# Turning the rounded values by 32x32 blocks and plain DMAs, and reordering the writes of one DMA queue, in an attention and int8 layer on one core

## The chip, the core and the metric

The kernel runs on one core of a Trainium2 chip. The core has a matrix engine (PE; its weight loads are shown as a separate row, PEld), a vector engine (DVE), a scalar engine (ACT), a general engine (POOL) and a sync engine (SP), which here only issues DMAs. Each works through its own queue in order, and they meet by semaphores. The metric is device microseconds of one execution; the value that counts is the median of several runs.

## The reference

The input is 16 sequences of 256 tokens with 256 features. Everything is float32. Two layers follow each other, each on a layer-normalised input and added back to its residual:

```
x = x + attention(layernorm(x))     # 16 heads of 128, 4 key/value heads
x = x + int8_linear(layernorm(x))   # 256 -> 256, with a bias
```

In the attention a query sees the first 4 tokens (the sink) and the last 32 (the window). In the linear layer each token's 256 values are divided by their largest absolute value over 127 and rounded to whole numbers; the weight's rows likewise; the product of the whole numbers is scaled back, and the bias is added.

## The kernel before

**Units.** The attention of one sequence `n` is cut into 8 units `(n, g, t)`: 4 key/value heads `g` by two halves `t` of the tokens. There are 128 units, and the main loop goes through them one after the other. Below, "unit k" is unit k of a sequence, k = 0 to 7; "unit 125" and the like counts over all 128. Inside a unit PE does the scores (`pss`, `L560`), some of the output projection of earlier units (`py`, `L678`), weights times values of the unit two before (`po`, `L623`), and then queries for units to come (`pq`, `L527`). In every even unit a "chunk" of keys or values for coming units stands ahead of the queries: keys (`pk`, `L495`) in units 4 and 0, values (`pv`, `L507`) in units 6 and 2. All engines' instructions stay in the order in which the program writes them (`in_written_order`).

**Seven products.** Queries, keys, values and output projections are made by a Strassen scheme: seven 128x128 products where eight would be plain (on PE each float32 product is two instructions). Four products go into one PSUM bank and three into another (`REGION`). `LARGE_FIRST` writes the bank of four first, `SMALL_FIRST` the bank of three. For keys and values the bank of four comes from the pool `m`, which has two buffers, and the bank of three is one of two query banks `q0`, `q1`. A query uses both query banks; the combination of its products on DVE (`L306` to `L310`) frees its first bank after `L307`. For keys and values ACT copies the bank of three out first, then the bank of four (`both_banks`, `L323`), and POOL combines the copies.

**Softmax weights.** DVE scales, masks and normalises the scores, turns them in 32x32 blocks (`L582`), and SP writes them to DRAM (`zd`, `L584`). At the begin of the next unit SP reads them back in another order (`ad`, `L588`); PE takes them in `po` one unit later. The first units and the last six do this turning on PE instead (`ptd`, `L565`), and PE then takes the result one unit later and not two (`lag`).

**Values.** POOL's combined values are written to DRAM (`vd`, `L512`) in the unit of the chunk, and read back from there in the next unit by three reads (`vw`, `L448` to `L453`).

**Inputs.** The normalised input of a coming sequence is turned in two steps (`turned_by_blocks`, `L385`): DVE turns 32x32 blocks, four DMAs write them to DRAM (`L394`), and one unit later four DMAs read them back in an order that completes the turn (`L403`).

**The linear layer.** `ffn_steps` (`L695`) makes a list of steps. The table `slots` (`L880`) says how many units after the end of the sequence's attention each is written, and it has a row of its own for sequence 14; sequence 15 is treated apart (`last_steps`). The steps are statistics, normalisation, scale, `quantise` (DVE multiplies and adds a large constant, POOL clips in `L724` and subtracts the constant with a bf16 result in `L725`), `turn` (one transposing DMA from bf16 to bf16, `L728`) and `linear` (four bf16 products `pa` on PE, `L739`; two DVE instructions, `L744`; a POOL addition, `L745`; the write of the result, `L746`). In a steady sequence `turn` stands in unit 1 and `linear` in unit 2.

**Where a step lands.** A step under `small` is written at the end of its unit; under `begin`, at the start, directly behind the issue of `ad`; under `later`, behind the unit's softmax. From unit 125 on the `small` steps are written earlier: on DVE ahead of the unit's normalisation (`L605` and on), on PE ahead of `po`. `close` belongs to the last unit.

Of the kernel before, what the change touches and what calls it, by code (L numbers as in the profile page):

```python
# [9 lines left out]
FP = mybir.dt.float32  # L10
BF = mybir.dt.bfloat16
AF = mybir.ActivationFunctionType
ALU = mybir.AluOpType
# [21 lines left out]
def kernel(  # L35
# [12 lines left out]
    pe, dve, act, pool, sp = nc.tensor, nc.vector, nc.scalar, nc.gpsimd, nc.sync  # L48
    B, T, DM = x.shape
    P = 128  # L50
# [4 lines left out]
    NC = DM // P  # L55
    NT = T // P
# [4 lines left out]
    QB = 32  # L61
# [9 lines left out]
    SCALE = 1.0 / math.sqrt(D)  # L71

    const = ctx.enter_context(tc.tile_pool(name="const", bufs=1))
    xp = ctx.enter_context(tc.tile_pool(name="xp", bufs=5))
    p1 = ctx.enter_context(tc.tile_pool(name="p1", bufs=1))
    p2 = ctx.enter_context(tc.tile_pool(name="p2", bufs=2))
    p3 = ctx.enter_context(tc.tile_pool(name="p3", bufs=3))
# [192 lines left out]
    def products(p, factors, order=LARGE_FIRST):  # L270

        a, sa, b, sb = factors
        pairs = {
            1: (a[0][0], b[0][0]), 2: (a[0][1], b[1][0]), 6: (sa[1], sb[1]), 7: (sa[2], sb[2]),
            4: (a[1][1], sb[3]), 5: (sa[0], sb[0]), 3: (sa[3], b[1][1]),
        }
        for i in order:
            yield region(p, i), *pairs[i]

    SMALL_FIRST = (4, 5, 3, 1, 2, 6, 7)
    turn_of = [0]

# [62 lines left out]
    def factors(n, w, sums, pair):  # L348

        a = [[w[:, c, (2 * pair + e) * D : (2 * pair + e + 1) * D] for c in range(NC)] for e in range(2)]  # L350
        return (
            a, [sums[:, i, pair % 2] for i in range(4)],
            xn_blocks(n), [xn_sums[n][:, i] for i in range(4)],
        )
# [27 lines left out]
        dve.tensor_copy(xnT[n], pt)  # L382
        channels(n)

    def turned_by_blocks(n):  # L385


        z = p1.tile([P, NQ, NT * NC, QB], FP, tag="zx", name=f"zx_{n}")
        dve.transpose(z, xns[n].rearrange("p t (c q i) -> p q (t c) i", c=NC, q=NQ))
        zd = dram.tile([P, NQ, NT * NC, QB], FP, tag="zx", name=f"zxd_{n}")  # L390

        def out():
            for a in range(NQ):
                sp.dma_start(  # L394
                    zd[:, a].rearrange("(q j) k i -> j q (k i)", q=NQ),
                    z[a * QB : (a + 1) * QB].rearrange("j q k i -> j q (k i)"),
                )

        def back():
            xnT[n] = p2.tile([P, NC, T], FP, tag="xnT", name=f"xnT_{n}")  # L400
            for t in range(NT):
                for c in range(NC):
                    sp.dma_start(  # L403
                        xnT[n][:, c, t * P : (t + 1) * P].rearrange("p (a i) -> p a i", a=NQ), zd[:, :, t * NC + c]
                    )

        return out, back

    NQ = P // QB
# [81 lines left out]
    def keys(n, pair):  # L491

        p = banks_of_chunk(f"pk_{n}_{pair}")
        for to, left, right in products(p, factors(n, wk_sb, wk_sums, pair), SMALL_FIRST):
            pe.matmul(to, left, right, start=True, stop=True)  # L495
        k = p1.tile([P, 2, 3, D], FP, tag="ktmp", name=f"ktmp_{n}_{pair}")
        kb = k[:, :, 0:2].rearrange("p e j (k i) -> p e (j k) i", i=QB)
        rest = lambda: keys_to(n, 2 * pair, kb)
        keys_late[rest] = 1 + pair
        return Products(p, f"k_{n}_{pair}", (k[:, 0, 0:3:2], k[:, 1, 2], k[:, 0, 1], k[:, 1, 0:2])), rest  # L500

    def values(n, pair):
        p = banks_of_chunk(f"pv_{n}_{pair}")

        order = LARGE_FIRST if (n, pair) == (1, 0) else SMALL_FIRST
        for to, left, right in products(p, factors(n, wv_sb, wv_sums, pair), order):
            pe.matmul(to, right, left, start=True, stop=True)  # L507
        v = p2.tile([P, 3, 2, D], FP, tag="vt", name=f"vt_{n}_{pair}")

        def rest():  # L510
            vd = dram.tile([T, 2 * D], FP, tag="vd", name=f"vd_{n}_{pair}")
            sp.dma_start(vd.rearrange("(j p) d -> p j d", p=P), v[:, 0:2].rearrange("p j e d -> p j (e d)"))  # L512
            values_buffer(n, pair)
            return lambda: values_to(n, pair, vd.rearrange("(b k) d -> b k d", k=QB))

        return Products(p, f"v_{n}_{pair}", (v[:, 0:3:2, 0], v[:, 2, 1], v[:, 1, 0], v[:, 0:2, 1])), rest
# [178 lines left out]
    def ffn_steps(n):  # L695
        xt = xts[n]
        tiles, tag = range(NT), f"{n}"
        h = p1.tile([P, NT, DM], FP, tag="h", name=f"h_{tag}")
        h16 = p1.tile([P, NT, DM], BF, tag="h16", name=f"h16_{tag}")
        xs = p2.tile([P, NT], FP, tag="xs", name=f"xs_{tag}")  # L700
        hT = p1.tile([P, NT, NC, P], BF, tag="hT", name=f"hT_{tag}")
        y = p1.tile([P, NT, DM], FP, tag="yo", name=f"y_{tag}")
        got = []

        def stats():
            got.append(statistics(xt, tiles, f"f{tag}"))

        def norm():
            standardise(h, xt, got[0], tiles)
            if n < B - 2:  # L710
                add_bias(pool)

        def scale():
            dve.tensor_reduce(xs, h, AX.X, ALU.max, apply_absolute_value=True)
            dve.tensor_scalar(xs, xs, 1.0 / 127.0, 1e-12, ALU.mult, ALU.max)

        def quantise():
            xr = p2.tile([P, NT], FP, tag="xr", name=f"xr_{tag}")
            dve.reciprocal(xr, xs)
            for j in tiles:  # L720
                dve.scalar_tensor_tensor(
                    h[:, j, :], h[:, j, :], xr[:, j : j + 1], magic.to_broadcast([P, DM]), ALU.mult, ALU.add
                )
            pool.tensor_scalar(h, h, MAGIC + 127.0, MAGIC - 128.0, ALU.min, ALU.max)  # L724
            pool.tensor_scalar(h16, h, MAGIC, None, ALU.subtract)  # L725

        def turn():
            sp.dma_start_transpose(  # L728
                hT.rearrange("p j c t -> p (j c) t"), h16.rearrange("p j d -> p (j d)")
            )  # L730

        def add_bias(eng):
            eng.tensor_add(xt, xt, bias_bc.unsqueeze(1).to_broadcast([P, NT, DM]))

        def linear():
            pa = ps_m.tile([P, NT, DM], FP, tag="m", name=f"pa_{tag}")
            for j in tiles:
                for c in range(NC):
                    pe.matmul(  # L739
                        pa[:, j, :], hT[:, j, c], wqfT[:, c, :],  # L740
                        start=(c == 0), stop=(c == NC - 1),
                    )
            for j in tiles:
                dve.scalar_tensor_tensor(y[:, j, :], pa[:, j, :], xs[:, j : j + 1], wsc_bc, ALU.mult, ALU.mult)  # L744
            pool.tensor_add(y, y, xt)  # L745
            sp.dma_start(out_v[n], y)  # L746

        return [stats, norm, scale, quantise, turn, linear, lambda: add_bias(dve)]

    def last_steps(j):  # L750

# [74 lines left out]
    def at(slot, f, what=small):  # L826
        what.setdefault(slot, []).append(f)
# [15 lines left out]
    for n in range(1, B):  # L843
        first = n * PER - 14
        places = (0, 1, 1, 2) if n == 1 else (4, 5, 6, 7) if n == 2 else (first - 2, first + 2, first + 4, first + 5)
        for k, slot in enumerate(places[:3]):
            at(slot, lambda n=n, k=k: norm_steps(n)[k]())
        if n == 1:
            at(places[3], lambda n=n: turned(n))
        else:  # L850
            def turn(n=n, slot=places[3]):
                for k, f in enumerate(turned_by_blocks(n)):
                    at(slot + 1 + k, f, begin)
                at(slot + 2, lambda: channels(n))

            at(places[3], turn)
            at(max(first - 4, 0), lambda n=n: load_x(n))
# [19 lines left out]
    for n in range(B - 1):  # L877
        done = (n + 1) * PER

        slots = (4, 5, 6, 8, 9, 10) if n < B - 2 else (4, 5, 6, 6, 7, 7, 7)  # L880
        for k, slot in enumerate(slots):
            def step(n=n, k=k):
                if k == 0:
                    steps[n] = ffn_steps(n)
                steps[n][k]()
            at(done + slot, step, begin if k == 4 and n == B - 2 else close if k == 5 and n == B - 2 else small)


    warm = ps_m.tile([P, P], FP, tag="m", name="warm")
# [25 lines left out]
    for i in range(len(units) + 2):  # L915
# [49 lines left out]
        if chunk:  # L965
            chunk.combine(pool)
            if chunk_rest in keys_late:
                at(i + keys_late[chunk_rest], chunk_rest, later)
            else:
                at(i + 1, chunk_rest(), later)  # L970
        for f in combined:
            if f:
                f()
# [44 lines left out]
```

## Time and profile before

| what | value |
|---|---|
| three runs | 767.9, 769.29, 769.09 us; median 769.09 us |
| the profiled execution | 767.44 us, of which 765.7 us lie between its first and last instruction (its span) |
| granted clock of PE | 0.997 of full speed |
| chain that ended last | 96% of the span on PE |

Eight consecutive units from the middle of the span, starting at 335.1 us: busy time of each engine, in us. The stretches are cut at tenths of a us.

| unit | PE | DVE | ACT | POOL | length |
|---|---|---|---|---|---|
| 0 | 6.30 | 5.43 | 3.17 | 2.86 | 6.3 |
| 1 | 5.10 | 4.72 | 2.30 | 4.63 | 5.1 |
| 2 | 6.70 | 4.61 | 3.74 | 6.34 | 6.7 |
| 3 | 5.10 | 4.68 | 3.17 | 3.63 | 5.1 |
| 4 | 6.40 | 5.98 | 3.17 | 4.09 | 6.4 |
| 5 | 5.10 | 4.02 | 2.79 | 3.69 | 5.1 |
| 6 | 6.30 | 5.97 | 3.85 | 4.16 | 6.3 |
| 7 | 5.10 | 3.87 | 2.30 | 2.75 | 5.1 |

A line of the timeline gives the start and the length in us, the engine, the line of the kernel, the operation, what it writes and reads, and how many equal instructions follow each other; in brackets stands idle time before it and what ended it. "SPq" are SP's DMA issues: their length is the time to issue, not to land. The chain of waits in order of time gives start, length and what it was.

### The profile page before, as it was taken

To read this page: it belongs to the slowest core of one execution; us is meant where nothing else is said; L and a number is where in the kernel's file an instruction comes from. 1 tells how busy PE (TensorE), PEld (TensorE's weight loads), DVE (VectorE), ACT (ScalarE), POOL (GpSimd) and SP (SyncE) were. 2 spreads that over 40 slices of the span, in tenths; PEclk is the share of its full clock that TensorE was granted. 3 is DMA by queue.
4 is the path that set the end of the run, shared out by engine and by line. 5 is a ranking of instruction groups with operands and counts; after the bars stand their busy time and mean duration, and the time that the engine had idled before them with its cause. 6 is when DMAs were issued, how large, how long until landed. Compare 5 with 4: busy or idle time off the path is not lost.

```text
span 765.7 us, 18824 instructions
## 1 busy us (share of the span) xinstructions
PE 754.4 (99%) x6483; PEld 742.4 (97%) x6483; DVE 621.8 (81%) x1775; ACT 399.2 (52%) x1561; POOL 511.7 (67%) x812
## 2 busy tenths in 40 slices
PE   9999999999999999999999999999999999999995
PEld 7999999999999999999999999999999999999994
DVE  2588888888888888888888888888888888778765
ACT  3555555555455454555555455554545555455551
POOL 4666977676675867757676675866758676675622
PEclk9999999999999999999999999999999999999998
DMA  7634354344544425445344543436344354443310
GB/s 241 215 102 129 106 147 140 107 124 118 154 124 133 131 90 163 128 137 144 100 125 128 147 141 123 129 96 163 120 145 135 99 136 128 130 137 105 100 40 31
DMA packets 150679, 97.45 MB, mean 127 GB/s; under 512 B 44984, under 2 KB 148792, under 8 KB 150584
## 3 DMA queue, kind: packets, MB, share of 16 engines
q1 hardware_dynamic: 150584, 96.24, 42.8%
q8 instruction: 52, 0.85, 0.5%
q14 instruction: 43, 0.35, 0.2%
HBM read 54.39 MB, written 39.85 MB: 123 GB/s over the span
## 4 chain that ended last, share of the span: by engine, by line
PE 96%; DVE 2%; DMA 1%; ACT 0%; POOL 0%; issue 0%; DVEq 0%; POOLq 0%; ACTq 0%
PE pq L527 24%; PE py L678 23%; PE po L623 15%; PE pss L560 14%; PE pk L495 6%; PE pv L507 6%; PE py L662 3%; PE pq L538 2%; PE pa L739 1%; DMA ad<-zd 1%; PE warm L891 1%; PE pv L470 0%; PE pk L461 0%; PE ptd L565 0%; ACT scores L598 0%
## 5 line engine op out<-in xcount | busy, mean ns | idle before, releaser
L598 ACT ACTIVATE scores<-scores,nmax 128x68 f32<-128x68 f32 x512 | 173.5, 340 | 247.2 <-DVE nmax L573 244.8
L623 PE MATMUL po<-ad,vw 96*128 96x128 f32 x1024 | 135.4, 275 | 0.4 <-DMA ad<-zd 0.4
L560 PE MATMUL pss<-kt,qt 128*128 128x68 f32 x1024 | 130.2, 268 | 0.0
L623 PEld LDWEIGHTS po<-ad,vw 96*128 96x128 f32 x1024 | 125.6, 192 | 1.5 <-DMA ad<-zd 0.5
L560 PEld LDWEIGHTS pss<-kt,qt 128*128 128x128 f32 x1024 | 126.1, 192 | 0.7 <-issue 0.5
L527 PE MATMUL pq<-xs,wq_sums 128*128 128x128 f32 x714 | 118.6, 275 | 0.0
L571 DVE SCALAR_TENSOR_TENSOR scores<-pss,masks 128x272 f32<-128x272 f32 x128 | 56.2, 439 | 63.7 <-PE pss L560 60.8
L527 PEld LDWEIGHTS pq<-xs,wq_sums 128*128 128x128 f32 x714 | 98.8, 192 | 0.0
L598 ACT ACTIVATION_READ_ACCUMULATOR scores<-scores,nmax 128x1 f32 x512 | 95.6, 187 | 0.0
L635 ACT COPY oT<-po 128x512 f32<-128x512 f32 x129 | 75.4, 585 | 23.0 <-PE po L623 23.0
L678 PE MATMUL py<-wo_sums,os 128*128 128x128 f32 x672 | 87.0, 279 | 0.0
L257 POOL TENSOR_TENSOR os<-oT 128x256 f32<-128x256 f32 x56 | 41.0, 732 | 58.0 <-ACT oT L635 58.0
L678 PEld LDWEIGHTS py<-wo_sums,os 128*128 128x128 f32 x672 | 79.5, 192 | 0.0
L306 POOL TENSOR_TENSOR ktmp<-b_k 128x256 f32<-128x256 f32 x30 | 22.4, 746 | 84.3 <-ACT b_k L327 84.3
L527 PE MATMUL pq<-xnT,wq_sb 128*128 128x128 f32 x476 | 72.7, 275 | 0.1
L582 DVE STREAM_TRANSPOSE z<-scores 128x384 f32<-128x384 f32 x120 | 69.4, 578 | 4.1
L617 DVE TENSOR_TENSOR scores<-scores,sm 128x272 f32<-128x272 f32 x120 | 60.3, 503 | 4.1
L527 PEld LDWEIGHTS pq<-xnT,wq_sb 128*128 128x128 f32 x476 | 62.7, 192 | 0.2 <-PE pv L507 0.2
L678 PE MATMUL py<-wo_sb,oT 128*128 128x128 f32 x448 | 62.0, 281 | 0.0
L573 DVE TENSOR_REDUCE nmax<-scores 128x4 f32<-128x272 f32 x128 | 55.8, 436 | 4.4
L678 PEld LDWEIGHTS py<-wo_sb,oT 128*128 128x128 f32 x448 | 54.5, 192 | 0.0
L308 DVE TENSOR_TENSOR qt<-pq,qt 128x256 f32<-128x256 f32 x119 | 50.5, 424 | 4.0
(187 smaller groups left out, 1700.4 us busy)
## 6 DMA issues: line engine op xcount, KB each, us to landing
zd<-z SPq DMA_DIRECT2D x120, 192.0 KB
ad<-zd SPq DMA_DIRECT2D x120, 192.0 KB
vd<-vt SPq DMA_DIRECT2D x30, 256.0 KB
vw<-vd SPq DMA_DIRECT2D x30, 256.0 KB
vw<-vd SPq DMA_DIRECT2D x30, 224.0 KB
x<-in_x_dram SPq DMA_DIRECT2D x15, 256.0 KB
out_dram<-y SPq DMA_DIRECT2D x15, 256.0 KB
zxd<-zx SPq DMA_DIRECT2D x56, 64.0 KB
```

The lines of the kernel that those rows point to most:

```text
L308: eng.tensor_add(c21_c22, like(p[1][:, 0:2], c21_c22), v.unsqueeze(1).to_broadcast(c21_c22.shape))
L495: pe.matmul(to, left, right, start=True, stop=True)
L527: pe.matmul(to, left, right, start=True, stop=True)
L560: pe.matmul(pss[:, k, :], qt[n, g][:, t, k].rearrange("p h i -> p (h i)"), kt[n, g][:, t * NBLK + k, :], start=True, stop=True,)
L571: dve.scalar_tensor_tensor(s[:, :, 0:NK], pss, SCALE, masks[:, t], ALU.mult, ALU.add)
L573: dve.tensor_reduce(nmax, s[:, :, 0:NK], AX.X, ALU.max, negate=True)
L582: dve.transpose(z, s.rearrange("p k (c i) -> p c k i", c=NCH))
L598: act.activation(s[:, k, 0:NK], s[:, k, 0:NK], AF.Exp, bias=nmax[:, k : k + 1], scale=1.0, accum_out=sm[:, k : k + 1],)
L617: dve.tensor_mul(s, s, sm.unsqueeze(2).to_broadcast([P, NBLK, NK]))
L623: pe.matmul(po[:, k], vw[n, g // 2][:, t * NBLK + k, g % 2 * D : (g % 2 + 1) * D], ad[:, :, k], start=True, stop=True,)
L635: act.copy(o[:, t, hs].rearrange("p h (k i) -> p k h i", i=QB), po[:, :, hs])
L678: pe.matmul(region(py, i), left[:, e], right[:, e], start=(g == 0 and e == 0 and i in (1, 4)), stop=(g == G - 1 and e == 1 and i in (7, 3)),)
```

## The change

For sequences 0 to 13 the rounded values are turned in the way that the inputs are: POOL leaves them in float32, DVE turns 32x32 blocks, four DMAs write and one unit later four read, and ACT narrows the result to bf16 (`narrow`). For sequence 14 PE turns them by four bf16 transposes, and ACT copies them out. The steps of the linear layer move: `turn` from unit 1 to unit 2, the DMAs to the begin of units 3 and 4, `narrow` to unit 5 and `linear` from unit 2 to unit 6. For sequence 13 each of these comes one unit earlier, so that its `linear` is in unit 125. The write of the result and the write of the values (`vd`) are issued at the begin of the unit after, behind that unit's `ad`. Keys of pair 0 (in unit 4, from sequence 2 on) are made `LARGE_FIRST`. The pool of input tiles gets a sixth buffer.

```diff
-    xp = ctx.enter_context(tc.tile_pool(name="xp", bufs=5))
+    xp = ctx.enter_context(tc.tile_pool(name="xp", bufs=6))
...
-    def turned_by_blocks(n):
+    def turned_by_blocks(src, pool_of, tag):
-        z = p1.tile([P, NQ, NT * NC, QB], FP, tag="zx", name=f"zx_{n}")
-        dve.transpose(z, xns[n].rearrange("p t (c q i) -> p q (t c) i", c=NC, q=NQ))
+        z = p1.tile([P, NQ, NT * NC, QB], FP, tag="zx", name=f"z_{tag}")
+        dve.transpose(z, src.rearrange("p t (c q i) -> p q (t c) i", c=NC, q=NQ))
...
-        for to, left, right in products(p, factors(n, wk_sb, wk_sums, pair), SMALL_FIRST):
+        order = LARGE_FIRST if n > 1 and pair == 0 else SMALL_FIRST
+        for to, left, right in products(p, factors(n, wk_sb, wk_sums, pair), order):
...
-        h16 = p1.tile([P, NT, DM], BF, tag="h16", name=f"h16_{tag}")
+        h16 = p1.tile([P, NT, DM], BF, tag="h16", name=f"h16_{tag}") if n == B - 2 else h
-        hT = p1.tile([P, NT, NC, P], BF, tag="hT", name=f"hT_{tag}")
+        hT = p1.tile([P, NC, T], BF, tag="hT", name=f"hT_{tag}")
...
+        way = []
+
         def turn():
-            sp.dma_start_transpose(
-                hT.rearrange("p j c t -> p (j c) t"), h16.rearrange("p j d -> p (j d)")
-            )
+            if n < B - 2:
+                way.extend(turned_by_blocks(h, p1, f"hb_{tag}"))
+                return
+            pt = ps_m.tile([P, NC, T], BF, tag="m", name=f"ht_{tag}")
+            for c in range(NC):
+                for j in tiles:
+                    pe.transpose(pt[:, c, j * P : (j + 1) * P], h16[:, j, c * P : (c + 1) * P], ident16)
+            way.append(pt)
+
+        def out():
+            way[0]()
+
+        def back():
+            way.append(way[1]())
+
+        def narrow():
+            act.copy(hT, way[-1])
...
-            for j in tiles:
-                dve.scalar_tensor_tensor(y[:, j, :], pa[:, j, :], xs[:, j : j + 1], wsc_bc, ALU.mult, ALU.mult)
-            pool.tensor_add(y, y, xt)
-            sp.dma_start(out_v[n], y)
-
-        return [stats, norm, scale, quantise, turn, linear, lambda: add_bias(dve)]
+
+            def rest():
+                for j in tiles:
+                    dve.scalar_tensor_tensor(y[:, j, :], pa[:, j, :], xs[:, j : j + 1], wsc_bc, ALU.mult, ALU.mult)
+                pool.tensor_add(y, y, xt)
+                return lambda: sp.dma_start(out_v[n], y)
+
+            return rest
+
+        if n < B - 2:
+            return [stats, norm, scale, quantise, turn, out, back, narrow, linear]
+        return [stats, norm, scale, quantise, turn, narrow, linear, lambda: add_bias(dve)]
...
-        slots = (4, 5, 6, 8, 9, 10) if n < B - 2 else (4, 5, 6, 6, 7, 7, 7)
+        slots = (4, 5, 6, 8, 10, 11, 12, 13, 14) if n < B - 2 else (4, 5, 6, 6, 7, 7, 7, 7)
+        if n == B - 3:
+            slots = (4, 5, 6, 8, 9, 10, 11, 12, 13)
         for k, slot in enumerate(slots):
-            def step(n=n, k=k):
+            def step(n=n, k=k, slot=done + slot):
                 if k == 0:
                     steps[n] = ffn_steps(n)
-                steps[n][k]()
-            at(done + slot, step, begin if k == 4 and n == B - 2 else close if k == 5 and n == B - 2 else small)
+                rest = steps[n][k]()
+                if rest:
+                    at(slot + 1, rest(), begin)
+            if n < B - 2:
+                at(done + slot, step, begin if k in (5, 6) else small)
+            else:
+                at(done + slot, step, begin if k == 4 else close if k == 6 else small)
...
             if chunk_rest in keys_late:
                 at(i + keys_late[chunk_rest], chunk_rest, later)
             else:
-                at(i + 1, chunk_rest(), later)
+                at(i + 1, lambda i=i, f=chunk_rest: at(i + 1, f(), later), begin)
```

More of the change, by code (lines that the diff above doesn't have):

```diff
@@ L383, in turned @@
         channels(n)
-    def turned_by_blocks(n):
-        z = p1.tile([P, NQ, NT * NC, QB], FP, tag="zx", name=f"zx_{n}")
-        dve.transpose(z, xns[n].rearrange("p t (c q i) -> p q (t c) i", c=NC, q=NQ))
-        zd = dram.tile([P, NQ, NT * NC, QB], FP, tag="zx", name=f"zxd_{n}")
+    def turned_by_blocks(src, pool_of, tag):
+        z = p1.tile([P, NQ, NT * NC, QB], FP, tag="zx", name=f"z_{tag}")
+        dve.transpose(z, src.rearrange("p t (c q i) -> p q (t c) i", c=NC, q=NQ))
+        zd = dram.tile([P, NQ, NT * NC, QB], FP, tag="zx", name=f"zd_{tag}")
         def out():
@@ L399, in back @@
         def back():
-            xnT[n] = p2.tile([P, NC, T], FP, tag="xnT", name=f"xnT_{n}")
+            to = pool_of.tile([P, NC, T], FP, tag=tag.split("_")[0], name=tag)
             for t in range(NT):
@@ L403, in back @@
                     sp.dma_start(
-                        xnT[n][:, c, t * P : (t + 1) * P].rearrange("p (a i) -> p a i", a=NQ), zd[:, :, t * NC + c]
+                        to[:, c, t * P : (t + 1) * P].rearrange("p (a i) -> p a i", a=NQ), zd[:, :, t * NC + c]
                     )
+            return to
         return out, back
@@ L739, in linear @@
                     pe.matmul(
-                        pa[:, j, :], hT[:, j, c], wqfT[:, c, :],
+                        pa[:, j, :], hT[:, c, j * P : (j + 1) * P], wqfT[:, c, :],
                         start=(c == 0), stop=(c == NC - 1),
                     )
-            for j in tiles:
-                dve.scalar_tensor_tensor(y[:, j, :], pa[:, j, :], xs[:, j : j + 1], wsc_bc, ALU.mult, ALU.mult)
-            pool.tensor_add(y, y, xt)
-            sp.dma_start(out_v[n], y)
-        return [stats, norm, scale, quantise, turn, linear, lambda: add_bias(dve)]
+            def rest():
[7 more added lines that the diff above has]
+        return [stats, norm, scale, quantise, turn, narrow, linear, lambda: add_bias(dve)]
     def last_steps(j):
@@ L851, in turn @@
             def turn(n=n, slot=places[3]):
-                for k, f in enumerate(turned_by_blocks(n)):
-                    at(slot + 1 + k, f, begin)
+                out, back = turned_by_blocks(xns[n], p2, f"xnT_{n}")
+                at(slot + 1, out, begin)
+                at(slot + 2, lambda: xnT.__setitem__(n, back()), begin)
                 at(slot + 2, lambda: channels(n))
```

## The prediction, made before the changed kernel was run

> **What bounds the kernel now.** I read the page's busy times first, then the chain that ended last, then the timelines of a steady sequence and of the last 40 us.
>
> ```profile
> PE 754.4 (99%) x6483; PEld 742.4 (97%) x6483; DVE 621.8 (81%) x1775; ACT 399.2 (52%) x1561; POOL 511.7 (67%) x812
> ```
> ```profile
> PE 96%; DVE 2%; DMA 1%; ACT 0%; POOL 0%; issue 0%; DVEq 0%; POOLq 0%; ACTq 0%
> ```
>
> PE is full. In the trace its float32 instructions of 128x128 start 112 ns apart, those of 128x256 216 ns, the bf16 products `pa` 109 ns, and a sequence repeats every 46.1 us. So only three things can move the time: PE instructions added or removed, gaps on PE, and the end, where DVE is last. I listed every start on PE that comes later than the usual distance from the one before. Between 85 and 737 us there are three kinds. One, 0.05 us in `py` (112 times), belongs to the code that stays. The second stands before `pk` in unit 4, in 12 sequences: the two starts are 0.039 and 0.072 us late, together 0.111 us, 1.33 us in all. The third occurs once:
>
> ```profile
> 169.25 1.84 PE py L678 x16
> 171.88 4.21 DMA ad<-zd
> ...
> 177.29 1.56 PE pk L495 x14
> ```
>
> This is the chain in order of time: `po` waited for the weights' read of unit 2, and started 0.62 us late at 176.14. SP's queue shows why that read was tight:
>
> ```profile
> 166.89 0.34 SPq L584 DMA_DIRECT2D zd<-z  x1
> 170.16 0.38 SPq L512 DMA_DIRECT2D vd<-vt  x1
> 171.40 0.38 SPq L746 DMA_DIRECT2D out_dram<-y  x1
> 171.88 0.41 SPq L588 DMA_DIRECT2D ad<-zd  x1
> ```
>
> `vd` waits for POOL's values and the result for POOL's addition; `ad` is queued behind both, 3.1 us after its `zd` had landed (166.89 + 1.92, the median landing). By the landing records `ad` takes 2.60 us (median of 120) and is back 2.9 to 4.6 us early in most units, but only 1.0 in unit 2 and 0.9 in unit 6, both behind `vd`. Four of 120 landed over 1 us later than the median (3.59, 3.94, 4.21, 4.50); one met a tight unit.
>
> **The change, part by part.**
>
> *Writes behind `ad`.* `vd` and the result go behind the next `ad`; units 2 and 6 then get the slack of the others. Gain 0.62 us in the profiled run. About 30 tight reads and 4 late ones in 120 make one hit of about 0.6 us an execution. `vw` is read one issue after `vd` either way, landing 3.5 to 3.8 us later, and is used units later. What is late next: nothing within 2.9 us on this queue.
>
> *Keys begin with the larger group.* Why `pk` waits:
>
> ```profile
> 361.05 0.29 DVE L307 TENSOR_TENSOR qt<-pq,qt 128x128 f32<-128x128 f32 x1
> 361.49 0.46 PE L495 MATMUL pk<-xs,wk_sb 128*128 128x128 f32 x2
> ...
> 384.34 0.39 PE L495 MATMUL pk<-xs,wk_sb 128*128 128x128 f32 x2
> ```
>
> The `pk` of unit 0 (384.34) takes 0.39 for the same two; in unit 4 DVE frees the query bank at 361.34, when PE already wants it. With the bank of four first this bank is wanted 8 x 0.112 = 0.90 us later, so the wait goes: -1.33 us. The other bank is from `m`, last copied out at 357.55. What is late next: the chunk's query bank is then finished last. ACT's copy of it starts 0.04 us after the products end and takes 0.48 (362.43), so it is free 14 x 0.112 + 0.16 (pipeline of the last) + 0.04 + 0.48 = 2.25 us after the first `pk`; the following `pq` loads for that bank 21 x 0.112 = 2.35 us after it. Cover 0.05 to 0.1 us, so this could cost between 0 and, if the copy is one ACT instruction (0.34) late, 14 x 0.24 = 3.4 us. I take 0, as ACT's last work before it ends at 362.23, 0.9 us ahead, and the copy would wait only for PE.
>
> *The turn in a steady sequence.* Added on PE: nothing (`pa` stays four products). DVE: one block transpose, 0.67 by its twin at `L389`, in unit 2 (4.61 busy of 6.7); the two `L744` (0.88) leave unit 2 for unit 6, where DVE idled 0.99 us before 377.12. ACT: `narrow`, 0.59 by the copy of the same size at `L635`, in unit 5 (2.79 of 5.1). POOL: `L725` now writes float32, 0.61 like `L724` and not 1.52. SP: four writes (1.95 us to issue, landing 2.78) begin unit 3, four reads (2.62, landing 2.63) unit 4, in place of one transposing DMA (1.25, landing 2.50). Queued behind them are that unit's `vd`, `zd` and the next `ad`; in the windows of units 3 and 4 SP has the room (354.2 to 356.2, 361.1 to 363.7), and `ad(3)`, `ad(4)` keep 3 us. So nothing; if the cover went, each read that is late by 1 us beyond it costs 1 us. The sixth input buffer costs no time.
>
> The DMA row invites a rule. By the Trainium skill, "DMA: Bandwidth & Descriptors", section "Rules for kernel authors", a transpose belongs to the hardware's DMA transpose and not to a plain DMA with a rearranged pattern, with a 19-fold difference. By that rule the eight DMAs would take some 47 us (an estimate, 19 x 2.50), `narrow` would be late and PE would wait in every sequence; the rows of the input's own turn (2.78 and 2.63) contradict it, and the sum goes by them.
>
> *The tail.* For sequence 13 `linear` moves from unit 122 to 125. The four `pa` (0.43) only move. Unlike in unit 122, its DVE steps now stand ahead of the normalisation:
>
> ```profile
> 735.23 0.72 DVE L193 TENSOR_SCALAR h<-x,mv_f 128x256 f32<-128x256 f32 x2
> 736.89 0.16 DVE L605 TENSOR_TENSOR sm<-sm,floor 128x4 f32<-128x4 f32 x1 [0.93 <-ACT scores L598]
> ...
> 737.30 0.69 DVE L611 TENSOR_TENSOR z<-scores,sm 128x384 f32<-128x384 f32 x1
> ```
> ```profile
> 737.34 1.06 PE L623 MATMUL po<-ad,vw 96*128 96x128 f32 x8
> ...
> 738.40 0.27 PE L565 MATMUL ptd<-ident,z 128*96 128x128 f32 x1
> ```
>
> Now `z` is ready at 737.99 and PE takes it at 738.40. After the change PE runs `pa` ahead of `po`, at 737.34, and DVE two `L744` behind it, ahead of this unit's two `L193` and the normalisation. The distance from `pa` to `L744` is shown for sequence 14:
>
> ```profile
> 749.19 0.60 PE L739 MATMUL pa<-wqfT,hT 128*128 128x256 bf16 x4
> 749.83 0.88 DVE L744 SCALAR_TENSOR_TENSOR y<-pa,xs,wsc_bc 128x256 f32<-128x256 f32 x2 [1.30 <-PE pa L739]
> ```
>
> From `pa`: 0.64 to `L744`, 0.79 for both (750.62 less 749.83), 0.65 for `L193`, 1.10 from `L605` to the end of `z`: 3.18 us, at 740.52. PE reaches `ptd` after 0.43 (`pa`), 0.89 (`po`) and 0.17 (`pss`), at 738.83. With 0.06 for the release: a gap of 1.75 us. Bounds 1.1 (should `L193` stand ahead) and 2.0 (the `L721` pair beside POOL takes 0.35 more than alone). PE has no gap from there to 752.7, and the last DVE chain hangs on `pa` of sequence 14 at 749.19, so it goes to the end one for one.
>
> Sequence 14 gets four bf16 transposes on PE: 4 x 0.055 to 4 x 0.11, I take 0.23. They want POOL's rounded values (done 744.80 here, PE is there at 744.84; both move with the gap): 0.1. `narrow` on ACT (idle after 747.20 but for one copy) is done before 749.
>
> A longer gap also asks for the clock. In the trace gaps of 0.62 and 1.22 us left the granted clock at 1.0, and only behind the last, 2.87 us, it fell to 0.5; 1.75 us lies nearer to the first two, so I add nothing, with +1.5 (3 us at half speed) as the upper end. The Trainium skill, "TensorE: Matmul & The Clock Gate", section "Why this matters for your kernels", says to keep PE from idling for more than about 3 us, one window of idleness being what halves the clock; by it 1.75 us would cost nothing, but the 2.87 us would be harmless too, and yet the clock fell 1.1 us behind them.
>
> *Sum.* 767.44 - 1.33 - 0.62 + 1.75 + 0.33 = 767.57 for an execution like the profiled one, which lies 1.65 below the median of 769.09 (runs 767.9, 769.29). That 1.65 stays but for late reads of units 2 and 6: the median run may have had more than the profiled one. Between 0 and 1.65 I take one more half hit, 0.3: 767.57 + 1.35 = **768.9 us**.
>
> **Rivals.** (About 0.2%, 1.54 us, is what a measurement of this kernel tells from no change.)
>
> *Faster: the gap at `ptd` is hidden, or the late reads make up most of the 1.65.* Either gives 768.9 - 1.75 = 767.2 or 768.9 - 1.35 = 767.6. For it: the runs differ by 1.4 us, about two hits. Against: the order on DVE is fixed as written. Chance 0.27.
>
> *Slower: `pq` waits for ACT's copy.* The cover is 0.05 to 0.1 us, 14 times. From a copy 0.2 us later than worked out (0.12 a time beyond the cover) it decides: 768.9 + 14 x 0.12 = 770.6; at 0.2 beyond, 771.7. For it: the cover is worked out from starts and ends that differ by hundredths, and is the smallest of all here. Against: in the trace the copy starts at once on its products. Chance 0.18.
>
> *Slower: SP's eight issues and their 0.5 MB a sequence delay `ad` in units 3 and 4.* Needs 3 us. If half of 28 reads lost 0.2: +2.8, 771.7. DMA engines are busy 0.34 and 0.56 there. Chance 0.07.
>
> *Keys don't do it.* If `pk` finds its `m` bank late instead: +1.33, 770.2, still no measurable change. Chance 0.08.
>
> *The forecast itself:* 0.40. Its own range is 768.0 to 770.0.
>
> **Numbers.** Faster 0.27. Same: 0.40 + 0.08. Slower 0.18 + 0.07. The range takes in 767.2 below and 771.4 above, between the two prices of the wait for ACT.
>
> **What would show it.** `pk` in unit 4 with 0.39 for its first two and no gap; `ad<-zd` of units 2 and 6 back 3 us or more early; on PE a gap of 1.75 us before `ptd` near 739; no wait at `pq` behind `pk`. A gap at `pq` of 0.1 us or more, or one of another length at 739, would prove me wrong.

## The result, and the profile after

The changed kernel takes 771.38 us (median of 20 executions, 769.2 to 775.36), the kernel before 768.47 on the same chip (20 executions, 767.74 to 771.18). The ratio is 1.0036, 95% interval 1.0022 to 1.0049: slower, where 768.9 and "no measurable change" were forecast. The executions of the changed kernel fall into groups: 8 lie between 769.20 and 770.06 with a mean granted clock of 0.997, 7 between 771.16 and 772.02 with 0.994 or 0.995, 5 between 774.04 and 775.36 with 0.990. One more interval of 3.41 us at half speed lowers this mean by 0.0022. The profiled one is of the last group: 774.17 us, span 772.4.

The lines of a trace are those of its own kernel: `L744`, `L739`, `L714`, `L715`, `L611`, `L565` of the kernel before are `L764`, `L757`, `L716`, `L717`, `L613`, `L567` of the changed one, and in an experiment they can stand a few lines further down (`L613` is `L616` in experiment 3).

The page of the changed kernel, its busy times and the engines of the chain that ended last:

```profile
PE 759.4 (98%) x6487; PEld 746.2 (97%) x6487; DVE 626.5 (81%) x1789; ACT 403.5 (52%) x1576; POOL 514.3 (67%) x812
PE 96%; DVE 2%; ACT 0%; POOL 0%; issue 0%; DVEq 0%; POOLq 0%; ACTq 0%
```

PE is as full as it was and has only four instructions more (the transposes of sequence 14), but 5.0 us more busy time: part of its work ran slower. The DMA share has left the chain: no late read any more. To find the place I took the first `pss` of each of the 128 units from both traces and compared the lengths of the units. The differences, in us (an evaluation of the trace, not a view of it):

```
                                           before    after
unit 4 of 12 sequences                      6.36      6.25    -0.11 each
unit 4 of sequence 3 (with the late read)   6.88      6.25    -0.62
unit 7 of 13 sequences                      5.14      5.25    +0.11 each
units 2 and 6 (pa moves)                    6.69/6.25 6.25/6.69
units 122 and 125 (pa of sequence 13)       6.69/5.05 6.25/5.48
unit 126                                    5.48     11.32    +5.84
unit 127 to the end                        21.96     23.60    +1.64
```

So the steady part is a draw with one late read saved, and the loss is at the end. DVE and the engines it meets in unit 125 and 126, in the timeline of the changed kernel:

```profile
736.15 0.60 PE L757 MATMUL pa<-wqfT,hT 128*128 128x256 bf16 x4
736.79 0.88 DVE L764 SCALAR_TENSOR_TENSOR y<-pa,xs,wsc_bc 128x256 f32<-128x256 f32 x2 [2.66 <-PE pa L757]
737.58 1.68 DVE L193 TENSOR_SCALAR h<-x,mv_f 128x256 f32<-128x256 f32 x2
737.75 1.36 POOL L765 TENSOR_TENSOR y<-y,x 128x512 f32<-128x512 f32 x1 [4.93 <-DVE y L764]
739.58 0.67 DVE L613 TENSOR_TENSOR z<-scores,sm 128x384 f32<-128x384 f32 x1
740.39 0.42 PE L567 MATMUL ptd<-ident,z 128*96 128x128 f32 x1 [2.57 <-DVE z L613]
742.22 1.06 PE L664 MATMUL py<-wo_sb,oT 128*128 128x256 f32 x2
```

Three things are to be seen. `L193` takes 1.68 us where it took 0.72, and ends when POOL's addition ends. PE's start of `ptd` is 2.73 us later than its usual distance (1.75 were forecast). And behind the gap PE's instructions are twice as long: `py` pairs take 1.06 and not 0.59, the distance from one to the next is 427 ns and not 216. The windows of the changed kernel give the granted clock; a line has the stretch, its length, busy time (and number) of PE, PEld, DVE, ACT and POOL, then the clock, the DMA share and GB/s:

```profile
736.00:738.00 2.00, 1.82 (x16) 1.52 (x14) 1.21 (x4) 0.26 (x1) 0.25 (x1) 1.00 0.00 0
...
742.00:744.00 2.00, 2.00 (x8) 1.64 (x8) 1.65 (x5) 1.32 (x6) 0.00 (x0) 0.50 0.00 0
744.00:746.00 2.00, 2.00 (x6) 1.61 (x5) 1.90 (x6) 0.71 (x5) 0.75 (x2) 0.50 0.00 0
```

The clock's records say 0.5 from 739.90 to 746.73 and again from 760.38 to 763.79: 6.83 and 3.41 us at half speed, some 5.1 us of lost PE work. That is the distance of the slowest group from the fastest (774.2 less 769.3). In every trace here the clock falls once more at the very end (at 760.87 in the kernel before, at 767.21 in the changed one), behind the last wait for `d_last`, when PE has only a few products left; this is why the mean is 0.997 and not 1 even in the fast group.

The two steps that were to gain did so. In unit 4 the keys now begin with the group of four, and the first four take 0.61, as everywhere; `pq` follows at the usual distance. SP issues `ad` 1.92 us after `zd`, ahead of `vd`:

```profile
360.31 0.61 PE L498 MATMUL pk<-xnT,wk_sb 128*128 128x128 f32 x4
...
361.64 0.39 PE L498 MATMUL pk<-xnT,wk_sums 128*128 128x128 f32 x2
361.87 0.61 PE L529 MATMUL pq<-xnT,wq_sb 128*128 128x128 f32 x4
```
```profile
166.71 0.34 SPq L586 DMA_DIRECT2D zd<-z  x1
168.63 0.30 SPq L590 DMA_DIRECT2D ad<-zd  x1
169.03 1.85 SPq L395 DMA_DIRECT2D zd_hb<-z_hb  x4
170.93 0.43 SPq L514 DMA_DIRECT2D vd<-vt  x1
```

By the landing records (an evaluation of the trace) the reads of units 2 and 6 come back 3.75 and 4.28 us early (medians of 15), those of units 3 and 4, which now have the eight DMAs beside them, 2.4 and 2.3, and none is waited for.

### The profile page after: what moved, and what is told of

Same layout as the page of the kernel before. It is cut to its first block, busy times and chain, and to the rows that moved or that the text cites. A ratio compares the mean times of both kernels' runs of the same rounds, so it can differ in the third digit from the quotient of the medians.

```text
span 772.4 us, 19024 instructions
## 1 busy us (share of the span) xinstructions
PE 759.4 (98%) x6487; PEld 746.2 (97%) x6487; DVE 626.5 (81%) x1789; ACT 403.5 (52%) x1576; POOL 514.3 (67%) x812
## 4 chain that ended last, share of the span: by engine, by line
PE 96%; DVE 2%; ACT 0%; POOL 0%; issue 0%; DVEq 0%; POOLq 0%; ACTq 0%
PE pq L529 24%; PE py L680 23%; PE po L625 14%; PE pss L562 14%; PE pk L498 6%; PE pv L509 6%; PE py L664 4%; PE pq L540 2%; PE pa L757 1%; PE ptd L567 1%; PE warm L923 1%; PE pv L472 0%; PE pk L463 0%; ACT scores L600 0%; DVE y L764 0%
## 5 line engine op out<-in xcount | busy, mean ns | idle before, releaser
L257 POOL TENSOR_TENSOR os<-oT 128x256 f32<-128x256 f32 x56 | 43.4, 776 | 58.0 <-ACT oT L637 58.0
```

## The experiments

**1. The addition beside `L193`.** My theory: POOL's addition and DVE's `L193` slow each other where they meet. For sequence 13 alone the addition is issued one unit later:

```diff
+                if n == B - 3:
+                    def add():
+                        pool.tensor_add(y, y, xt)
+                        return lambda: sp.dma_start(out_v[n], y)
+                    return add
                 pool.tensor_add(y, y, xt)
...
-                if rest:
+                if rest and n == B - 3:
+                    add = rest()
+                    at(slot + 1, lambda: at(slot + 2, add(), begin))
+                elif rest:
                     at(slot + 1, rest(), begin)
```

> POOL's addition of sequence 13 (1.36 us, 737.75 to 739.11 in the changed kernel's trace) is issued one unit later, behind POOL's work of sequence 14; nothing else moves. Theory A (the addition beside them stretches DVE's two L193 from 0.72 to 1.68 us): L193 takes 0.7 again, the gap on PE before ptd near 740 shrinks from 2.73 to about 1.75 us. Rival (L193 is slow in this place whatever POOL does): 1.6 and 2.7 stay. Theory C (the clock halves because PE idles more than some 2 us): with 1.75 us the clock stays at 1.0 behind the gap, so that every execution lies within 0.5 us of about 768.4, against three groups (769.3, 771.5, 774) for the changed kernel. Rival to C (the clock falls for another reason): it still falls in some executions, by 2 to 5 us.

Measured: 770.13 us (768.24 to 770.47), ratio 1.0021 (1.0012 to 1.0031). In its timeline `L193` is short again, with nothing on POOL beside it:

```profile
736.91 0.88 DVE L764 SCALAR_TENSOR_TENSOR y<-pa,xs,wsc_bc 128x256 f32<-128x256 f32 x2 [2.66 <-PE pa L757]
737.70 0.73 DVE L193 TENSOR_SCALAR h<-x,mv_f 128x256 f32<-128x256 f32 x2
739.56 0.29 PE L567 MATMUL ptd<-ident,z 128*96 128x128 f32 x1 [1.62 <-DVE z L613]
```

The start of `ptd` is 1.79 us late; the prediction's sum had 1.75. Theory A holds, and the sum was short by this overlap alone. Behind this gap the clock stays at 1.0. But the executions do not lie in one group: in the profiled one the clock falls at 756.27, behind the wait for `d_last` at the end, for one stretch of 3.41 us. Six of the nine executions lie between 769.96 and 770.47 with a mean clock of 0.994 or 0.995, and only the fastest, 768.24, lies where all were expected. That part of the expectation failed.

**2. The normalisation first.** The linear step of sequence 13 is written behind the normalisation of sequence 14 in unit 125:

```diff
+            if n == B - 3 and k == 8:
+                last_linear = done + slot, step
-            if n < B - 2:
+            elif n < B - 2:
                 at(done + slot, step, begin if k in (5, 6) else small)
...
+    at(*last_linear)
```

> In unit 125 the linear step of sequence 13 stands behind the normalisation of sequence 14, so that L193 runs while DVE waits for pa; nothing else moves. By the sum of the prediction (its lower bound) the gap on PE before ptd is then 1.1 us. If the dose of idleness decides on the clock, it stays at 1.0, and executions lie near 769.3 - 2.73 + 1.1 = 767.7. If POOL's addition now stretches the normalisation's DVE instructions in place of L193, the gap is 1.4 to 2.0 us and the time 768.0 to 768.6.

Measured: 770.28 us (768.86 to 771.19), ratio 1.0024 (1.0013 to 1.0035). `L193` now runs in the idle time, and the addition meets the next DVE instruction:

```profile
738.61 1.26 POOL L765 TENSOR_TENSOR y<-y,x 128x512 f32<-128x512 f32 x1 [4.96 <-DVE sm L607]
738.64 0.18 DVE L608 RECIPROCAL sm<-sm 128x4 f32<-128x4 f32 x1
738.85 1.55 DVE L613 TENSOR_TENSOR z<-scores,sm 128x384 f32<-128x384 f32 x1
740.55 0.29 PE L567 MATMUL ptd<-ident,z 128*96 128x128 f32 x1 [1.86 <-DVE z L613]
```

`L613` takes 1.55 where it took 0.67, and the gap is 2.02 and not 1.1. Both runs together show the overlap from two sides: the DVE instruction that stands beside the addition pays 0.9 us, and `L608` beside it pays nothing. The Trainium skill says so ("SBUF — State Buffer", section "Who interferes with whom"): DVE and POOL share one pair of ports, which one instruction holds to its end, and on DVE a `tensor_scalar` in a fast mode or an instruction with two inputs in SBUF needs it, one with a single input outside these modes does not. `L193` (ending 0.15 us behind the addition), `L613` and `L608` (0.18) agree with that; that `L193` runs in a fast mode is not shown by any run. The half clock follows at 741.20, for one stretch of 3.41 us. Two of the seven executions, 768.86 and 768.91, kept a mean clock of 0.997, the others lie between 770.18 and 771.19.

**3. The gap filled with idle work.** 21 transposes of the identity on PE inside the gap; nothing else changes:

```diff
+            if w == units[-3] and k == 0:
+                for _ in range(21):
+                    pe.transpose(ptd[:, 0:P], ident[:, 0:NKP], ident)
             if w:
                 pe.transpose(ptd[:, k * P : (k + 1) * P], sw[:, k]...
```

> The changed kernel with 21 transposes of the identity on PE (about 2.3 us, results overwritten) in the gap before the first ptd of unit 126; every other instruction and wait stays. Theory C: ptd starts as late as in the changed kernel, 2.7 us after the first pss, but PE was not idle, so the clock stays at 1.0 and every execution lies at 769.2 to 769.8. Rival (the clock falls for another reason than idleness): the executions spread over 769 to 775 as before, and half speed is seen between 740 and 747 in some.

Measured: 769.28 us, ratio 1.0017 (1.0008 to 1.0026). Nine of 11 executions lie between 769.04 and 769.79, two at 771.0; none above. In the timeline `ptd` is as late as in the changed kernel, and in the windows the clock is 1.00 where it was 0.50:

```profile
738.12 2.46 PE L568 MATMUL ptd<-ident 128*96 128x128 f32 x21
740.80 0.31 PE L570 MATMUL ptd<-ident,z 128*96 128x128 f32 x1 [0.22 <-DVE z L616]
```
```profile
742.00:744.00 2.00, 2.00 (x11) 1.75 (x10) 1.86 (x6) 1.68 (x8) 0.00 (x0) 1.00 0.00 0
```

So it is PE's idleness that lowers the clock there: with PE kept busy the same gap costs 1.5 us less (ratio 1.0036 to 1.0017). The two executions at 771.0 were not expected. I put them to the other place, as in experiment 1, but only the clock's mean (0.994, 0.995: one interval at half speed more) speaks for it.

**4. `linear` of sequence 13 in unit 124,** where its DVE steps stand behind the normalisation:

```diff
-            slots = (4, 5, 6, 8, 9, 10, 11, 12, 13)
+            slots = (4, 5, 6, 8, 9, 10, 11, 11, 12)
```

> The linear step of sequence 13 in unit 124 (narrow in 123), where the steps still stand behind the unit's normalisation; nothing else moves. Theory: no gap before ptd of unit 126, no half clock there, all executions near 769.3 - 2.7 = 766.6. What is left against the kernel before is then one group, at about 0.998 of it. Rival (the tail was already waiting for something else, so that the gap hid it): less than 1.5 us comes back, and a new gap stands behind 740.

Measured: 766.95 us (766.78 to 767.68), ratio 0.9984 (0.9975 to 0.9992). Almost nothing is left of the gap:

```profile
737.89 0.28 PE L567 MATMUL ptd<-ident,z 128*96 128x128 f32 x1 [0.18 <-DVE z L613]
```

This start is 0.34 us later than its usual distance, and no gap at all was expected; 0.34 is also what lies between the 766.6 expected and the 766.95 measured. No execution has the longer times, and the clock falls once, at 759.17, in the last products. The whole loss against the kernel before was this placing.

**5. The scale ahead of `linear` in unit 6.** Where the 0.11 us in unit 7 come from is seen on DVE in the changed kernel:

```profile
375.46 0.88 DVE L764 SCALAR_TENSOR_TENSOR y<-pa,xs,wsc_bc 128x256 f32<-128x256 f32 x2 [1.60 <-PE pa L757]
376.25 0.67 DVE L716 TENSOR_REDUCE xs<-h 128x2 f32<-128x512 f32 x1
376.96 0.20 DVE L717 TENSOR_SCALAR xs<-xs 128x2 f32<-128x2 f32 x1
377.08 0.43 DVE L573 SCALAR_TENSOR_TENSOR scores<-pss,masks 128x272 f32<-128x272 f32 x1
```

The scale of the next sequence (`L716`, `L717`), which the kernel before did while DVE waited anyway, is queued behind `L764`, which waits 1.60 us for `pa`. The scores of unit 7 begin 1.82 us after its first `pss` (375.26) and not 1.04, the query combination ends later, and `pq` waits for its banks: the first four of unit 7 take 0.63 where 0.61 is usual, and two behind them 0.46 and not 0.39.

```profile
378.83 0.63 PE L529 MATMUL pq<-xnT,wq_sb 128*128 128x128 f32 x4
...
379.76 0.46 PE L529 MATMUL pq<-xs,wq_sb 128*128 128x128 f32 x2
```

The edit registers the linear steps of sequences 0 to 12 after all scales:

```diff
-    steps = {}
+    steps, linears = {}, []
...
+            if n < B - 3 and k == 8:
+                linears.append((done + slot, step))
-            if n < B - 2:
+            elif n < B - 2:
                 at(done + slot, step, begin if k in (5, 6) else small)
...
+    for slot_and_step in linears:
+        at(*slot_and_step)
```

> In unit 6 the scale of the next sequence (L716, L717) stands ahead of the linear step (pa, L764) for sequences 0 to 12; nothing else moves. Theory: the waits of 0.11 us at pq in unit 7 come from L716 being queued behind L764, which waits 1.6 us for pa, so that the scores of unit 7 start 0.78 us late. With L716 in that idle time the waits go: unit 7 of a steady sequence takes 5.14 and not 5.25 us, 13 x 0.11 = 1.4 us less in all. Rival (the two L764 alone are too much for the start of unit 7): unit 7 stays at 5.2 us or more. The spread of the tail (769, 771, 774) stays, less 1.4.

Measured: 771.52 us (769.56 to 771.79), ratio 1.0035 (1.0023 to 1.0047). Unit 7 takes 5.14 in the trace and a steady sequence 46.00 and not 46.10. Its DVE lines:

```profile
373.38 0.68 DVE L716 TENSOR_REDUCE xs<-h 128x2 f32<-128x512 f32 x1
...
375.06 0.88 DVE L764 SCALAR_TENSOR_TENSOR y<-pa,xs,wsc_bc 128x256 f32<-128x256 f32 x2 [0.59 <-PE pa L757]
375.91 0.44 DVE L573 SCALAR_TENSOR_TENSOR scores<-pss,masks 128x272 f32<-128x272 f32 x1
```

The scores begin 1.05 us after the first `pss` (374.86). The order was the cause, not the two `L764`. The time alone would not have shown it: the tail is as it was, and its spread is larger than 1.4 us. In the profiled execution the clock falls at 740.38 and at 757.45, for 3.41 us each; four of the five executions lie at 771.50 to 771.79 with the same mean clock, 0.992. Less these two stretches (3.4 us) that is 768.1, against 769.20 to 770.06 for the changed kernel's group without them. Of the groups expected at about 768, 770 and 773 only the middle one is seen, once (769.56): by the mean clock none of the five executions was without half clock.

**6. The keys alone,** on the kernel before:

```diff
-        for to, left, right in products(p, factors(n, wk_sb, wk_sums, pair), SMALL_FIRST):
+        order = LARGE_FIRST if n > 1 and pair == 0 else SMALL_FIRST
+        for to, left, right in products(p, factors(n, wk_sb, wk_sums, pair), order):
```

> The kernel before with only the keys of unit 4 beginning with the larger group. Theory: the 12 waits of 0.11 us before pk in unit 4 go and none comes at pq behind it: unit 4 takes 6.25 and not 6.36 us, 1.3 us less in all. Rival (pq then waits for ACT's copy of the other bank, cover 0.05 to 0.1 us): unit 4 stays at 6.3 us or more, no gain.

Measured: 767.07 us (765.15 to 768.41), ratio 0.9980 (0.9972 to 0.9989). Unit 4 takes 6.25, and no `pq` waits behind it:

```profile
360.17 0.61 PE L496 MATMUL pk<-xnT,wk_sb 128*128 128x128 f32 x4
...
361.07 0.39 PE L496 MATMUL pk<-xs,wk_sb 128*128 128x128 f32 x2
...
361.74 0.61 PE L528 MATMUL pq<-xnT,wq_sb 128*128 128x128 f32 x4
```

**7. The writes alone,** on the kernel before:

```diff
-                at(i + 1, chunk_rest(), later)
+                at(i + 1, lambda i=i, f=chunk_rest: at(i + 1, f(), later), begin)
...
-            sp.dma_start(out_v[n], y)
+            return lambda: sp.dma_start(out_v[n], y)
...
-                steps[n][k]()
+                rest = steps[n][k]()
+                if rest:
+                    at(slot + 1, rest, begin)
```

> The kernel before with only the writes of values and results issued behind the next ad. Theory: the reads of units 2 and 6 come back 3 us or more early and not 0.9, PE never waits for a late one: 0 to 1.2 us less, and a smaller spread of the executions. Rival: vw lands too late for po, since its read is issued behind a later write, or another ad is the tight one: a gap on PE at po, time as before or longer.

Measured: 766.46 us, ratio 0.9971 (0.9961 to 0.9981): 2.2 us less than the 768.62 of the kernel before, measured with it. The read is issued 1.92 us after `zd`, ahead of both writes:

```profile
167.03 0.34 SPq L584 DMA_DIRECT2D zd<-z  x1
168.95 0.30 SPq L588 DMA_DIRECT2D ad<-zd  x1
170.30 0.38 SPq L512 DMA_DIRECT2D vd<-vt  x1
171.53 0.40 SPq L746 DMA_DIRECT2D out_dram<-y  x1
```

The eight executions lie within 0.37 us (766.26 to 766.63), the 20 of the kernel before within 3.0 (767.12 to 770.12). The expectation had 0 to 1.2. So late reads seem to cost most executions of the kernel before far more than the 0.62 us that its profiled one shows. No slow execution of it was traced, so this is inferred from what goes with its cause. Experiment 6, whose writes stand as before, speaks for it: its profiled execution, in which PE waits for no late read, is its fastest, 765.15 us, as fast as experiment 8 below, while its median is 767.07.

**8. Keys and writes,** both edits on the kernel before:

> The kernel before with both edits (keys with the larger group first, writes behind ad) and without the turn by blocks. If the two gains add up: 1.3 + 0.6 = 1.9 us less, 766.6 where the kernel before has 768.5, ratio 0.9975, faster than both kernels. If they hide one another: 1.3.

Measured: 765.37 us (764.87 to 765.59), ratio 0.9958 (0.9946 to 0.9970). The two gains nearly add up (1.3 by the trace and 2.2 by the times; 3.2 together), and this beats both kernels. The expectation of 1.9 was short by the same late reads.

**9. The changed kernel mended,** with the edits of experiments 4 and 5:

> The changed kernel with the scale ahead of the linear step in unit 6 and the linear step of sequence 13 in unit 124, so the turn by blocks without the two waits that it came with. If these two waits and the clock behind the second are all that it costs, it lies at 766.95 - 1.4 = 765.5, level with the kernel before with keys and writes changed alone (765.37). Rival (the turn's eight DMAs, the block transpose or the four PE transposes cost something by themselves): 766.0 or more.

Measured: 765.74 us (765.23 to 766.13), ratio 0.9963 (0.9949 to 0.9977). It is level with experiment 8 within the uncertainty (each ratio is known to 0.0012 to 0.0014 either way, which makes some 1.4 us for their difference; the kernel before lay at 768.4 to 768.7 in every set of runs). A steady sequence takes 46.00 us in both traces. So no cost and no gain of the turn by blocks and DMAs itself is seen; one under some 1.4 us is not excluded.

**10. What idleness does to the clock.** Experiment 7's kernel with idle DVE work that makes PE wait at `pk` in unit 4:

```diff
+        for _ in range(IDLE.get(i, 0)):
+            dve.scalar_tensor_tensor(spare, spare, 1.0, spare, ALU.mult, ALU.max)
         if waiting:
             waiting.combine(dve)
```

> The kernel before with the writes behind ad, and 3 to 8 idle DVE instructions (0.40 us each, on a spare tile) ahead of the query combination in unit 4 of sequences 2 to 13, so that PE waits 1.3, 1.7, 2.1, 2.5, 2.9, 3.3 us at pk, twice each. Theory C (the clock is set every 3.41 us by PE's idleness in the window that ended, on a grid that falls differently in each execution): the half clock follows in steps of 3.41 us from one boundary, behind most gaps of 2.5 us and more, behind some of 1.7 to 2.1 us and none of 1.3. Rival 1 (an idle gap of over 3 us is needed): behind the two of 3.3 only. Rival 2 (idleness has nothing to do with it): behind none.

> The same with 4, 5, 6 and 7 idle DVE instructions, three times each: gaps of 1.7, 2.1, 2.5 and 2.9 us. Theory C: the windows with 1.5 us of idle or more are followed by half clock, those with less are not, whatever the length of the gap that they cut; so of the three gaps of one length some are followed and some not. Rival 1: none. Rival 2: none.

Measured: 827.08 and 826.58 us, with 24 gaps of 2.15 to 4.45 us; they came out longer than meant, some 0.46 us an instruction on top of about 0.8. A gap of the first kernel that is followed by half clock, and one that is longer and is not, in its timeline:

```profile
133.13 0.46 PE L495 MATMUL pk<-xs,wk_sb 128*128 128x128 f32 x2 [2.15 <-DVE qt L307]
...
490.32 0.46 PE L495 MATMUL pk<-xs,wk_sb 128*128 128x128 f32 x2 [2.61 <-DVE qt L307]
```

In every trace of this study all changes of the granted clock lie on a grid of 3.413 us (distances between them are multiples to within 0.01), whose place differs from execution to execution. The idle time of PE in each interval of the grid that began at full clock and holds part of a gap at `pk` in these two kernels (an evaluation of the traces):

```
followed by half clock in the next interval:  1.96 1.99 2.06 2.15 2.15 2.18 2.23 2.25 2.61 2.71 2.83 and more
not followed (0.3 us and more):               0.35 0.37 0.51 0.63 0.84 1.09 1.11 1.16 1.29 1.35 1.35 1.37 1.70 1.77
```

The gap of 2.15 us lay in one interval and was followed; the gap of 2.61 was cut into 0.84 and 1.77 and was not, nor one of 3.07 in the second kernel (1.37 and 1.70). Both rivals fall; the limit is between 1.77 and 1.96 us of idle time in an interval here, not the 1.5 of the expectation. The gap of experiment 2 (1.86 in its interval, followed) lies between. At the end of the program it is less clean: intervals with 1.49 to 1.55 us idle were followed in the changed kernel and experiments 1 and 5; those with 1.43 and 1.44 in experiments 4, 6, 7 and 9 were not, and neither were one with 1.62 in experiment 9 and one with 1.92 in experiment 6. What else counts there stays open.

## Why the prediction was wrong

Both signs that the prediction named against itself came: a wait of 0.11 us at `pq`, though in unit 7 and not behind `pk`, and a gap of another length near 739. That the median of 771.38 lies just inside the stated range is luck: its upper end, 771.4, was set between two prices of a wait for ACT that did not occur.

- **Keys: right.** -1.33 us was forecast; the trace shows 0.11 in 12 sequences, and experiment 6 confirms it. The narrow cover at the following `pq` held, so the rival with ACT's copy did not come about.
- **Writes behind `ad`: mechanism right, size too small.** The term was 0.62 for the profiled execution and "one more half hit, 0.3" for the median run. Removing the cause gave 2.2 us (interval 1.5 to 3.0). The step that failed is the estimate of one hit an execution from four late landings in 120 of a single trace (by the landing records 3.69 and 3.74 belong to them too, which still makes only one and a half hits); the spread of the times, which I put down as a rival with a chance of 0.27, was the better sign.
- **The turn in a steady sequence: "nothing" was right, as far as experiment 9 can tell, for DMAs, block transpose and ACT, wrong for `L744` in unit 6.** I saw 0.99 us of idle time there and costed the two instructions at nothing, without asking what is queued behind an instruction that waits: `L716` and `L717`. Price 13 x 0.11 = 1.4 us (experiment 5), the whole gain of the keys.
- **The tail: place and mechanism right, size short by 0.98.** The forecast 1.75 is what comes out when the addition is moved away (1.79, experiment 1). The step that failed is the term `L193`, 0.65: it left out that POOL adds beside it, and the pair took 0.96 more (1.68 and not 0.72). Only the upper bound of 2.0 allowed for POOL, with the 0.35 of the `L721` pair. The lower bound of 1.1 failed for the same reason: with `L193` ahead the addition meets `L613`, and the gap is 2.02 (experiment 2).
- **The clock: "so I add nothing" failed.** Whether the clock falls depends on the gap's length and its place on the grid (experiment 10); in 12 of 20 executions of the changed kernel the mean clock is lower and the time 2 to 6 us longer.
- **Sequence 14 on PE: right.** Four transposes take 0.22 us, the wait before them is 0.02 to 0.05.

The terms with their measured sizes: 766.46 (experiment 7, late reads gone) - 1.33 + 1.4 + 2.73 + 0.25 = 769.5, and the group of the changed kernel without half clock lies at 769.20 to 770.06. The rest to the median of 771.38 is put to the clock: 1.9 us, where one interval at half speed costs 1.7 (unit 126 of experiment 2 is 3.72 us longer than in the kernel before, of which the gap is 2.02). The errors partly cancel: the writes gained 1.3 us more than the 0.92 that the sum gave them, and without that the miss would have been larger.

The rule of the Trainium skill that the prediction cited ("TensorE: Matmul & The Clock Gate", "Why this matters for your kernels": no gap beyond about 3 us) is too generous for what these runs show: 2.57 us of waiting, and 2.15 in experiment 10, were enough.

## What to carry to other kernels

Where a step is moved into an engine's idle time, ask what stands behind it in that queue while it waits; idle time in front of an instruction is only free if nothing else was using it (`L716` and `L717` were). On a core whose matrix engine is full, price a new gap by its length plus the clock: from some 2 us on in mid-program (at the end here 1.5 us of idle time in an interval were sometimes enough), the half clock that can follow costs 1.7 us for each 3.41 us interval, and whether it follows changes from execution to execution, so look at the group of times and not only at the median. A read that is tight in one profile may be late in other executions, and the spread of their times tells more of it than the one hit that the profile happens to hold.

## What I had not expected of the hardware

- The granted clock changes only on a grid of 3.413 us that starts somewhere else in each execution; in the two kernels of experiment 10 an interval with 1.96 us or more of idle PE in the middle of the program was always followed by half clock, one with 1.77 or less never.
- A DVE instruction beside POOL's addition of 128x512 (1.26 to 1.38 us) was lengthened by 0.9 to 1.0 us: the pair `L193` from 0.72 to 1.68, `L613` from 0.67 to 1.55, while `L608` beside it kept its 0.18.
